# Four small stores and one large load, in place of one large store and four small loads, in a block exchange through DRAM

## The chip, the cores and the metric

The kernel runs on one core of a Trainium2 chip. The metric is the time of the device for one execution, in microseconds (us), the median of several executions. The core has a matrix engine (TensorE, in the profile PE, its weight loads PEld), a vector engine (VectorE, DVE), a scalar engine (ScalarE, ACT), a general engine (GpSimd, POOL) and a queue engine (SyncE, SP), which only issues transfers here. Each of them works through its own instructions strictly in their written order and waits at semaphores for the others. Transfers (DMAs) run on 16 DMA engines of the core, shared by all queues.

## The reference

One transformer block: attention with normalised queries and keys, and then a mixture of experts in which each expert takes its best 512 tokens. Cut to what matters, for `x` of shape 16 x 256 x 256 (batches, tokens, width) and 16 heads of 64:

```python
shift = silu(t) @ W_ada.T + b_ada
h = ln(x, ln1_g, ln1_b) + shift
qkv = (h @ Wqkv.T).reshape(b, n, 3, H, HD)
q = ln(qkv[:, :, 0].transpose(0, 2, 1, 3), qn_g, qn_b)
k = ln(qkv[:, :, 1].transpose(0, 2, 1, 3), kn_g, kn_b)
v = qkv[:, :, 2].transpose(0, 2, 1, 3)
attn = softmax(einsum('bhnd,bhmd->bhnm', q, k) / sqrt(HD))
o = einsum('bhnm,bhmd->bhnd', attn, v)
x = x + o.transpose(0, 2, 1, 3).reshape(b, n, H * HD) @ Wout.T
tok = x.reshape(-1, d)
gate = softmax(tok @ Wgate.T)
vals, idx = top_k(gate.T, bs // E)          # 8 experts, 512 tokens each
g = ln(tok[idx.T], mlp_g, mlp_b)
y = gelu(einsum('ked,ehd->keh', g, fc1s) + b1s)
y = (einsum('keh,edh->ked', y, fc2s) + b2s) * vals.T[..., None]
tok = tok.at[idx.T].add(y)
```

All of it is float32.

## The kernel before

The attention takes the 16 batches one after the other, in a software pipeline with a period of 48.3 us; the mixture of experts follows. In a batch, `First` normalises `x` and transposes it, twelve `Group`s (six column groups of the projection, two halves of the tokens) make queries, keys and values, eight `Quad`s (pairs of head pairs, `d`, each with two steps `i`) do the attention, and two `Tail`s the output projection, the residual, the stores of the tokens and the gate.

Two things have to be transposed between partitions and columns: the normalised keys (`qk` to `kT`) and the softmax rows (`pr` to `prT`). In the first and the last batch (`DIRECT`) TensorE does it. In the 14 batches between, VectorE and the DMA engines do it together, in three steps that the change touches:

- `turn`: VectorE's stream transpose turns each 32 x 32 block within its group of 32 partitions, from `pr` to `pb` (L832; for keys from `qk` to `kb`, L749). Two such instructions fill one tile of 128 partitions by 4 KB, 512 KB in all. The tags `pb` of both kinds share three buffers.
- `away`: SyncE stores the tile to a block in DRAM (`blocks`, L840; `kblocks`, L756).
- `back`: SyncE loads it from there so that the block of rows group `k` and column group `q` ends in row group `q` and column group `k`: four loads, one for each group of 32 partitions, into `prT` (L854) or `kT` (L764).

A batch has eight such exchanges of softmax rows and two of keys: 14 x 8 = 112 and 14 x 2 = 28 in all. Afterwards ScalarE applies gain and bias to the keys in place (`affine`, L770) and TensorE uses them for the scores (L794); `prT` goes into the product with the values (L881).

The order of the work is written out. Each step is added to a `Plan` with an engine; the long list `PLACES` holds a due place for each step, made with an estimate of 0.36 us of SyncE for `away` and 1.6 us for `back`, and the steps are emitted in the order of these numbers. So the order of each engine's instructions is fixed, and each waits for what it needs when its turn comes. SyncE's list holds, beside the exchange, the load of the next batch's `x` (`load_x`, L537, five buffers), the stores of the tokens (`out<-tok`, L918) and of the normalised tokens (`xn_dram<-tn`, L928). VectorE's list holds the statistics of the loaded `x` (`st<-xs`, L610) between the transposes, maxima and scalings of other batches. A transfer that SyncE issues uses one of eight semaphores in turn, so an issue also waits until the transfer eight places before it has landed.

## Time and profile before

| | us |
|---|---|
| median of 3 runs | 1104.83 (1104.45 to 1106.43) |
| profiled execution, whole time | 1106.04 |
| profiled execution, span from first to last instruction | 1104.2 |

| engine | busy us | share of the span |
|---|---|---|
| TensorE, matrix products | 1070.6 | 97% |
| TensorE, weight loads | 714.8 | 65% |
| VectorE | 778.9 | 71% |
| GpSimd | 616.2 | 56% |
| ScalarE | 596.1 | 54% |

The attention takes the first 780 us or so, the selection of the tokens about 60 us, the experts the rest. The granted TensorE clock is 0.99 on average. In the profile's page, a group of instructions is told by its line and by the names of what it writes and reads (`prT<-blocks`). The view of waits sums up, for each engine and line, the idle time just before the instruction and what ended it ("DVE st L610 <- DMA xs<-in_x: 14.2, 5, 3.9": us in total, times, longest). The view by windows gives the busy time of each engine within a stretch, and at the end of a line the granted clock, the mean busy share of the 16 DMA engines and GB/s. The timeline lists instructions in order of time, several alike merged into one row, with idle time and its cause in brackets; times are counted from the start of the span.

### The profile page before, as it was taken

To read this page: it belongs to the slowest core of one execution; us is meant where nothing else is said; L and a number is where in the kernel's file an instruction comes from. 1 tells how busy PE (TensorE), PEld (TensorE's weight loads), DVE (VectorE), ACT (ScalarE), POOL (GpSimd) and SP (SyncE) were. 2 spreads that over 40 slices of the span, in tenths; PEclk is the share of its full clock that TensorE was granted. 3 is DMA by queue.
4 is the path that set the end of the run, shared out by engine and by line. 5 is a ranking of instruction groups with operands and counts; after the bars stand their busy time and mean duration, and the time that the engine had idled before them with its cause. 6 is when DMAs were issued, how large, how long until landed. Compare 5 with 4: busy or idle time off the path is not lost. (4 is left out here: it accounts for less than half of the span.)

```text
span 1104.2 us, 18872 instructions
## 1 busy us (share of the span) xinstructions
PE 1070.6 (97%) x5835; PEld 714.8 (65%) x5835; DVE 778.9 (71%) x2201; ACT 596.1 (54%) x1656; POOL 616.2 (56%) x997
## 2 busy tenths in 40 slices
PE   7999999999999999999899999999988999999996
PEld 4555656566565655656465655656767888888885
DVE  6657888777778777786678787676568488654540
ACT  2768666565766566566557667576522333322331
POOL 3766776776676665675657666565411233333332
PEclk9999999999999999999999999999999999999998
DMA  6013998785888787796787778895130456555661
GB/s 211 1 39 123 277 259 237 230 255 166 248 260 227 226 246 234 201 260 211 211 251 227 228 224 240 243 256 179 63 102 20 113 189 200 170 162 175 196 201 19
DMA packets 147539, 209.20 MB, mean 189 GB/s; under 512 B 15088, under 2 KB 122864, under 8 KB 147440
## 3 DMA queue, kind: packets, MB, share of 16 engines
q1 hardware_dynamic: 139520, 197.71, 60.0%
q0 software_dynamic: 6144, 8.39, 4.1%
q10 hardware_dynamic: 1776, 1.90, 0.5%
q8 instruction: 47, 0.77, 0.3%
q14 instruction: 52, 0.43, 0.1%
HBM read 121.96 MB, written 85.98 MB: 188 GB/s over the span
## 5 line engine op out<-in xcount | busy, mean ns | idle before, releaser
L683 PE MATMUL pm<-wq,hT 128*128 128x512 f32 x768 | 360.4, 605 | 5.0 <-DVE qk L716 2.8
L822 POOL TENSOR_SCALAR pr<-pr,sums 128x256 f32<-128x256 f32 x512 | 237.1, 481 | 112.2 <-DVE sums L818 92.9
L811 ACT ACTIVATE pr<-sc,nmax 128x256 f32<-128x256 f32 x512 | 238.0, 480 | 97.5 <-DVE nmax L802 80.3
L683 PEld LDWEIGHTS pm<-wq,hT 128*128 128x128 f32 x768 | 137.3, 192 | 146.1 <-issue 131.1
L103 POOL TENSOR_TENSOR ss<-ss,neghalf 128x8 f32<-128x8 f32 x128 | 210.5, 1645 | 10.6
L802 DVE TENSOR_REDUCE nmax<-sc 128x2 f32<-128x512 f32 x256 | 165.3, 676 | 16.9 <-PE sc L794 16.3
L832 DVE STREAM_TRANSPOSE pb<-pr 128x512 f32<-128x512 f32 x224 | 149.9, 690 | 18.5 <-POOL pr L822 13.6
L794 PE MATMUL sc<-kT,qT 64*128 64x256 f32 x1024 | 135.4, 397 | 0.0
L881 PE MATMUL po<-prT,v 128*64 128x256 f32 x1024 | 127.6, 388 | 1.1 <-DVE gates L950 1.1
L700 DVE TENSOR_REDUCE ss<-sq 128x8 f32<-128x512 f32 x128 | 86.0, 672 | 47.3 <-ACT sq L696 46.8
L794 PEld LDWEIGHTS sc<-kT,qT 64*128 64x128 f32 x1024 | 92.8, 188 | 40.8 <-issue 25.4
L696 ACT ACTIVATE sq<-pm 128x512 f32<-128x512 f32 x128 | 76.9, 603 | 77.3 <-PE pm L683 75.9
L1301 POOL DMA_INDIRECT out<-y,idx x32 | 51.2, 1601 | 119.8 <-DVE y L1295 66.9
L1268 PE MATMUL ph<-xT,w 128*128 128x256 f32 x512 | 117.6, 383 | 0.0
L907 PE MATMUL pw<-wo,oT 128*128 128x256 f32 x512 | 116.6, 381 | 0.3 <-DVE qk L716 0.3
L1284 PE MATMUL py<-w,hid 128*128 128x256 f32 x512 | 116.3, 380 | 0.0
L716 DVE TENSOR_TENSOR qk<-pm,ss 128x512 f32<-128x512 f32 x128 | 87.0, 681 | 36.9 <-POOL ss L103 35.9
L907 PEld LDWEIGHTS pw<-wo,oT 128*128 128x128 f32 x512 | 96.0, 190 | 23.2 <-issue 9.4
L811 ACT ACTIVATION_READ_ACCUMULATOR pr<-sc,nmax 128x1 f32 x512 | 107.6, 210 | 0.0
L881 PEld LDWEIGHTS po<-prT,v 128*64 128x64 f32 x1024 | 67.1, 137 | 61.5 <-issue 21.1
L1275 ACT ACTIVATE hid<-ph,vec 128x256 f32<-128x256 f32 x128 | 60.4, 474 | 84.2 <-PE ph L1268 76.3
L1284 PEld LDWEIGHTS py<-w,hid 128*128 128x128 f32 x512 | 95.6, 190 | 12.8
(140 smaller groups left out, 1132.6 us busy)
## 6 DMA issues: line engine op xcount, KB each, us to landing
blocks<-pb SPq DMA_DIRECT2D x112, 512.0 KB
prT<-blocks SPq DMA_DIRECT2D x448, 128.0 KB
w<-in_fc2T SPq DMA_DIRECT2D x16, 1024.0 KB
w<-in_fc1T SPq DMA_DIRECT2D x16, 1024.0 KB
kblocks<-kb SPq DMA_DIRECT2D x28, 512.0 KB
kT<-kblocks SPq DMA_DIRECT2D x112, 128.0 KB
out<-tok SPq DMA_DIRECT2D x32, 128.0 KB
xn_dram<-tn SPq DMA_DIRECT2D x32, 128.0 KB
```

Source lines behind the costliest of these rows:

```text
L103: nc.gpsimd.tensor_tensor(dst, src, neghalf[:, : src.shape[1]], ALU.pow)
L683: nc.tensor.matmul(self.pm, hTs[self.b][:, c, bass.ts(self.t, P)], wq[:, c, bass.ts(self.g, GW)], start=(c == 0), stop=(c == DC - 1),)
L716: engine.tensor_tensor(self.qk.rearrange("p (h d) -> p h d", d=HD), src.rearrange("p (h d) -> p h d", d=HD), self.ss[:, 1, :].unsqueeze(2) ...
L794: nc.tensor.matmul(self.sc[i, j][:, t, :], qTs[self.b][rows, hp, bass.ts(t, P)], keys[rows, hp] if direct else keys[rows, hp // 4, hp % 4] ...
L802: nc.vector.tensor_reduce(self.nmax[i, j], self.sc[i, j], AX.X, ALU.max, negate=True)
L811: nc.scalar.activation(self.pr[i, j][:, t, :], self.sc[i, j][:, t, :], AF.Exp, bias=self.nmax[i, j][:, t : t + 1], scale=1.0, accum_out=se ...
L822: nc.gpsimd.tensor_scalar(self.pr[i, j][:, t, :], self.pr[i, j][:, t, :], self.sums[i][:, 1, j, t : t + 1], 1.0, ALU.mult, ALU.mult,)
L832: nc.vector.transpose(self.pb[i][:, :, :, j].rearrange("p k c t n -> p t k c n"), self.pr[i, j].rearrange("p t (k c m) -> p t k c m", c=TB ...
L881: nc.tensor.matmul(self.po[j * HD : (j + 1) * HD, i, :], vs[self.b][:, c, bass.ts(4 * self.d + 2 * i + j, HD)], prT[:, j, c] if self.b in ...
L907: nc.tensor.matmul(self.pw, oTs[self.b][:, hp // 2, self.t, hp % 2, :], wo[:, hp, :], start=(hp == 0), stop=(hp == HP - 1),)
L1268: nc.tensor.matmul(self.ph[f], self.w1[:, c, bass.ts(f, P)], self.xT[:, c, :], start=(c == 0), stop=(c == DC - 1),)
L1284: nc.tensor.matmul(self.py[i], self.hid[:, f, bass.ts(i, P)], self.w2[:, f, :], start=(f == 0), stop=(f == FC - 1),)
```

## The change

The block in DRAM has its dimensions laid out in another order: by the partition that will read it, not by the one that writes it. The shape of the tile stays the same (4 x 32 x 4 x 256 floats). Before, a store writes the 128 partitions one after the other, each 4 KB in one piece, and each of four loads takes for 32 partitions four pieces of 1 KB, 4 KB apart. After, each of four stores writes, for one group of 32 partitions, four pieces of 1 KB that lie 128 KB apart (and 4 KB from the next partition's), and one load reads 128 partitions, each 4 KB in one piece. Both kinds of exchange are changed alike. The planner's numbers and `PLACES` stay, so the order of the steps stays on every engine; within a step of SyncE, `away` has now four transfers and `back` one.

```diff
--- before.py
+++ after.py
@@ -753,17 +753,17 @@
 
             def away(self, kb):
                 self.blocks = dram.tile([QB, SQ, QB, N], F32, tag="blocks", bufs=4, name="kblocks")
+                for k in range(QB):
+                    nc.sync.dma_start(
+                        self.blocks[:, :, k].rearrange("q d n -> d q n"),
+                        kb[0][bass.ts(k, SQ)].rearrange("p q t h m -> p q (t h m)"),
+                    )
+
+            def back(self):
                 nc.sync.dma_start(
-                    self.blocks.rearrange("k d q n -> (k d) (q n)"),
-                    kb[0].rearrange("p q t h m -> p (q t h m)"),
-                )
-
-            def back(self):
-                kT = self.keys()[:, self.g - 2].rearrange("p k t h m -> p k (t h m)")
-                for q in range(QB):
-                    nc.sync.dma_start(
-                        kT[bass.ts(q, SQ)], self.blocks[:, :, q].rearrange("k d n -> d k n")
-                    )
+                    self.keys()[:, self.g - 2].rearrange("p k t h m -> p (k t h m)"),
+                    self.blocks.rearrange("q d k n -> (q d) (k n)"),
+                )
 
             def affine(self):
                 kT = self.keys()[:, self.g - 2].rearrange("p k t h m -> p (k t h m)")
@@ -837,10 +837,11 @@
             def away(self, i):
 
                 self.blocks[i] = dram.tile([QB, SQ, QB, N], F32, tag="blocks", bufs=4, name="blocks")
-                nc.sync.dma_start(
-                    self.blocks[i].rearrange("k m q n -> (k m) (q n)"),
-                    self.pb[i].rearrange("p q c h t n -> p (q c h t n)"),
-                )
+                for k in range(QB):
+                    nc.sync.dma_start(
+                        self.blocks[i][:, :, k].rearrange("q m n -> m q n"),
+                        self.pb[i][bass.ts(k, SQ)].rearrange("p q c h t n -> p q (c h t n)"),
+                    )
 
             def turned(self, i):
                 if i not in self.prT:
@@ -849,11 +850,9 @@
 
             def back(self, i):
 
-                prT = self.turned(i).rearrange("p (k n) -> p k n", k=QB)
-                for q in range(QB):
-                    nc.sync.dma_start(
-                        prT[bass.ts(q, SQ)], self.blocks[i][:, :, q].rearrange("k m n -> m k n")
-                    )
+                nc.sync.dma_start(
+                    self.turned(i), self.blocks[i].rearrange("q m k n -> (q m) (k n)")
+                )
 
             def transposes(self, i, j):
                 self.pp[i, j] = ps.tile([P, TB, N], F32, tag="sc", bufs=4, name="pp")
```

## The prediction

> **What bounds the kernel now.** I read the page's busy table and its slices first, then TensorE's waits, then the tiles of the exchange, and last SyncE's order in time around the few long waits. The page:

> ```profile
> PE 1070.6 (97%) x5835; PEld 714.8 (65%) x5835; DVE 778.9 (71%) x2201; ACT 596.1 (54%) x1656; POOL 616.2 (56%) x997
> DMA  6013998785888787796787778895130456555661
> q1 hardware_dynamic: 139520, 197.71, 60.0%
> q0 software_dynamic: 6144, 8.39, 4.1%
> ```

> TensorE is busy for 97% of the span, so shorter transfers gain only what it still loses to waits; but the 16 DMA engines are 70 to 90% busy in most slices of the attention (to about 780 us), so the changed queue is not idle either. The exchange ends in `prT` (read by TensorE, L881) and `kT` (read by ScalarE, L770). In the view of tile `prT`, the list of what the engines sat idle for has only

> ```profile
>   DMA prT<-blocks: 1.2, 4
>   DMA kblocks<-kb: 0.8, 1
> ```

> that is 2.0 us in 112 + 28 exchanges. By the trace's landing marks (the semaphore updates of each transfer) set against the first read, every `prT` is there at least 2.1 us before its product, half of them over 9.6 us. The exchange itself is covered. What is not covered is a load that the change does not name. VectorE's waits:

> ```profile
> DVE st L610 <- DMA xs<-in_x: 14.2, 5, 3.9
> ```

> The next batch's `x` (L537) is issued by the same SyncE queue, often right behind exchange stores. The timeline of one such place, batch 11's load:

> ```profile
> 419.29 0.34 SPq L756 DMA_DIRECT2D kblocks<-kb  x1
> 419.67 1.27 SPq L840 DMA_DIRECT2D blocks<-pb  x2
> 421.04 1.15 SPq L537 DMA_DIRECT2D xs<-in_x  x1
> ...
> 427.37 0.43 DVE L610 BATCH_NORM_STATS2 st<-xs 128x6 f32<-128x256 f32 x1 [2.06 <-DMA xs<-in_x]
> ...
> 429.25 0.47 ACT L811 ACTIVATE pr<-sc,nmax 128x256 f32<-128x256 f32 x1 [2.04 <-DVE pb L832]
> ...
> 430.58 0.61 PE L944 MATMUL pl<-wg,tokT 128*128 128x8 f32 x4 [1.52 <-ACT tokT L939]
> ```

> Three stores, then the load; VectorE stands 2.06 us for it with two transposes into `pb` queued behind; ScalarE waits 2.04 us for the `pr` that these free; TensorE loses 1.52 us. This is the bound that the change touches.

> **The change, part by part.**

> *Issue on SyncE.* Each exchange keeps five DMAs. Four loads in a row take 1.76 us from first to last (71.63, `kT`), twelve take 5.54 (341.76): 0.46 each. A single store takes 0.34 to 0.43. So each store's place on the queue grows from 0.4 to 1.85 us (+1.4), and each load's shrinks as much. Over a whole exchange SyncE is unchanged; whatever stands between store and load is moved 1.4 us later for each exchange store ahead of it.

> *DMA work.* In windows that hold one kind of transfer, share times length gives its cost in time of all 16 engines:

> ```profile
> 69.70:71.40 1.70, 1.70 (x5) 0.76 (x4) 0.00 (x0) 1.31 (x4) 1.62 (x4) 1.00 0.75 308
> 72.40:75.40 3.00, 3.00 (x15) 1.71 (x14) 1.59 (x3) 1.36 (x3) 2.44 (x4) 1.00 0.62 175
> 272.20:272.90 0.70, 0.70 (x9) 0.35 (x6) 0.70 (x2) 0.00 (x0) 0.62 (x2) 1.00 0.52 187
> ```

> (the last two columns are DMA share and GB/s.) The 512 KB store in 4 KB pieces: 0.75 x 1.70 = 1.28 us. Four loads in 1 KB pieces: 0.62 x 3.00 = 1.86. A 128 KB store in 1 KB pieces (`xn_dram`): 0.52 x 0.70 = 0.36, four of them 1.46. One exchange goes from 3.14 to 1.46 + 1.28 = 2.74 us. The new stores read 32 partitions and write every fourth kilobyte, which no row shows; the lower bound is 1.46, the upper the four loads' 1.86, which have that shape the other way round (3.14: no change). A still dearer price is the last rival. I take 1.46: same direction, same piece.

> *Length of one exchange.* Before: 2.64 us from store to released load (68.99 to 71.63), then 1.76 us of issue and some 2.7 us until the last load's marks: 7.1. After: 1.85 of issue, with 1.3 us from the last store's issue to its landing (marks of lone 128 KB stores: 1.70 from start of issue); then one load, 0.4 + 2.2 + about 0.9 for its further data: 6.7. Within 0.5 us of before, against 2.1 us of cover: nothing for the products. For `kT`, seven of 28 affines stand within 0.2 us of the landing, but scores follow them 0.3 us or more later in all but one. I take -0.5 us for all of this and keep 0 to -2.0.

> [...]

> *Waits.* The product waits for one landing, not four; the load on SyncE and the next VectorE transpose into that `pb` for four, not one. A semaphore instruction takes 21 ns on VectorE and changes no gap between its instructions in the trace: 0. The first products of groups with four landings start after the same 93 ns gap as the direct batches': 0 on TensorE too.

> *What stands behind the stores: the `x` loads.* In batches 9, 10, 12 and 15 no store is directly ahead; in 6 a store and four loads are (now 0.5 us earlier); in 7 and 14 one store (+0.6 and +1.3, slack 0.9 and 2.3). That leaves four:

> - Batch 11: `kblocks` at 419.29, now twelve stores, 5.5 us, so `x` is issued at 424.8, not 421.04. It then landed 6.33 us after issue, because three 512 KB stores were ahead in the DMA engines; now SyncE hands over 0.36 us of work every 0.46 us, so the engines keep up. Lone `x` loads land 2.8 to 3.3 us after issue by the marks, the median of all is 3.7. I take 2.8 to 3.7: 427.6 to 428.5, later by 0.2 to 1.1.
> - Batch 13: `kblocks` at 519.04, same pattern, VectorE released at 527.15: later by 0.2 to 1.1.
> - Batch 8: 275.92, twelve stores and an `out` store, issue at 281.9, landing 284.7 to 285.6 against 283.39: later by 1.3 to 2.2.
> - Batch 5: 131.38, eight stores, issue at 135.1, landing 137.9 to 138.8, against a start of the statistics at 137.19: a new wait of 0.7 to 1.6.

> *From VectorE to TensorE.* The three waits of before, 2.05, 2.06 and 3.94 us, cost TensorE 0.50, 1.52 and 0.56 + 2.23 us: on average the first 1.1 us is absorbed and the rest passes. In batches 8, 11 and 13 the absorbing part is used up, so the addition, 1.7 to 4.4 us, passes whole; batch 5 passes 0 to 0.5. Sum: 1.7 to 4.9, middle 3.3.

> *Sum.* +3.3 - 0.5 = +2.8 us. The profiled execution is 1104.2 of span and 1106.04 in all; it becomes 1108.8. It stands 1.2 above the median of the runs shown, so the median goes from 1104.83 to 1107.6; I say 1107.6.

> **The rivals.**

> - *Covered anyway.* The additions in 11 and 13 come out at their low end and VectorE's lost time is won back at later slack: +0.5 us, 1105.3. For it: the waits are few, and TensorE's stalls total about 10 us in the whole attention. Against: the three existing waits each show in TensorE.
> - *Faster: the queue empties.* The same pacing that delays issue leaves the DMA engines free, the work falls by 0.4 us an exchange, and `x` lands sooner than now. It decides where issue to landing stays under about 2.5 us; then the waits of 11 and 13 shrink, and with the 2.0 us of exchange waits gone the time is about 1102.5, at most 4.8 + 2.0 less: 1098. Against it: no `x` load in the trace lands in under 2.78 us.
> - *Slower by far: 1 KB stores are dear.* The software queue's packets average 4.1% x 16 x 1104.2 / 6144 = 118 ns; if a piece cost that, four stores would take 3.8 us, an exchange 5.1, ten of them 51 us in a batch of 48.3 us. The DMA engines would set the pace: with 0.80 of 48 us used now, some 58 us a batch, over 100 us in all. It decides above about 87 ns a piece (9.4 us free a batch, over ten exchanges of 512 pieces on 16 engines). Against: 1 KB stores on this queue take 0.36 x 16 / 128 = 45 ns.

> [...]

> **How the numbers follow.** Forecast as summed 0.56; covered 0.22; faster 0.15; dear stores 0.07. Differences of under 0.2% (2.2 us) can hardly be measured here. The forecast's own range is 1106 to 1110, a sixth of it within 0.2%. Slower 0.46 + 0.03 + 0.07 = 0.56; same 0.10 + 0.18 + 0.03 = 0.31; faster 0.13. (The covered case gives 0.03 to slower and 0.01 to faster, the faster one 0.03 to the same.) The range goes from 1102.0, just under the faster rival's 1102.5, up to 1112.5, which takes a partial version of the dear stores (TensorE losing the upper 4.9 and `kT` late as well).

> **What would show it.** Right: SyncE rows of four `blocks` stores in 1.8 us; `x` issued near 424.8 and 524.5; VectorE's wait for `xs` up from 14.2 to 17 to 20 us in one more place; TensorE's stalls behind it; DMA busy share of the hardware queue down from 60 to about 55%. Wrong: `xs` waits unchanged or less; packets of the new stores above 60 ns; a `prT` that TensorE waits for.

## The result and the profile after

The changed kernel takes 1116.05 us (median of 4 runs, 1115.19 to 1118.14) against 1105.63 us of the kernel before in the same comparison (4 runs): ratio 1.0097, 95% interval 1.0079 to 1.0116, that is 10.4 us slower. The profiled execution took 1115.93 us, with a span of 1114.0 us (before 1104.2).

The page of the changed kernel, the lines that answer to those shown of before:

```profile
PE 1073.8 (96%) x5835; PEld 714.8 (64%) x5835; DVE 780.6 (70%) x2201; ACT 596.1 (54%) x1656; POOL 618.3 (55%) x997
DMA  6014888785777686777787787876211466556661
q1 hardware_dynamic: 139520, 197.71, 57.8%
```

The DMA engines have less to do: the hardware queue fell from 60.0% of a span of 1104.2 us to 57.8% of one of 1114.0. In time of all 16 engines that is 19 us less, an estimate from these two shares. So the stores in 1 KB pieces are not dear for the DMA engines. TensorE does the same work and is busy 3.2 us longer. The tile `prT` still hides (the list of what the engines sat idle for):

```profile
  DMA blocks<-pb: 1.3, 3
  DMA kblocks<-kb: 0.8, 1
```

The loss shows in the waits (engine, instruction, what it waited for: us in total, times, longest):

```profile
DVE st L610 <- DMA xs<-in_x: 21.8, 7, 5.3
ACT kT L770 <- DMA kT<-kblocks: 16.7, 8, 3.3
DVE pb L832 <- DMA blocks<-pb: 4.8, 7, 1.5
PE pl L943 <- ACT tokT L938: 3.4, 1, 3.4
DVE kb L749 <- DMA blocks<-pb: 2.7, 1, 2.7
PE pl L943 <- DVE gates L949: 2.6, 1, 2.6
```

Before, the first was 14.2 (5 times), and of the others there were

```profile
ACT kT L770 <- DMA kT<-kblocks: 2.5, 3, 1.4
DVE pb L832 <- DMA blocks<-pb: 3.7, 2, 3.2
PE pl L944 <- ACT tokT L939: 1.5, 1, 1.5
```

Two transfers are later than before: the next batch's `x`, as predicted, and the keys' `kT`, to which the prediction had given a small gain. Batch 11's `x` load, the place that the prediction showed:

```profile
425.87 1.77 SPq L757 DMA_DIRECT2D kblocks<-kb  x4
...
427.68 4.02 SPq L841 DMA_DIRECT2D blocks<-pb  x8
...
431.81 0.40 SPq L537 DMA_DIRECT2D xs<-in_x  x1
...
435.41 0.43 DVE L610 BATCH_NORM_STATS2 st<-xs 128x6 f32<-128x256 f32 x1 [3.92 <-DMA xs<-in_x]
...
437.29 0.47 ACT L811 ACTIVATE pr<-sc,nmax 128x256 f32<-128x256 f32 x1 [3.90 <-DVE pb L832]
...
438.63 0.61 PE L943 MATMUL pl<-wg,tokT 128*128 128x8 f32 x4 [3.38 <-ACT tokT L938]
```

Twelve issues take 5.8 us where three took 1.6; the load follows, lands 3.6 us later, and the chain is the one of before with every wait longer. And then comes something that no row of the prediction had: after the pause TensorE runs at half clock. Windows of the same trace (from and to, length, busy time of TensorE, weight loads, VectorE, ScalarE, GpSimd, then the granted clock, DMA share, GB/s):

```profile
286.60:290.04 3.44, 1.65 (x12) 1.21 (x12) 3.32 (x12) 0.59 (x1) 2.23 (x6) 1.00 0.90 291
290.04:293.45 3.41, 3.29 (x16) 1.69 (x16) 3.40 (x8) 2.59 (x9) 3.14 (x5) 0.50 0.96 325
436.80:440.20 3.40, 1.57 (x7) 1.10 (x8) 3.40 (x10) 2.91 (x8) 2.99 (x8) 1.00 0.56 149
440.23:443.64 3.41, 3.41 (x12) 1.20 (x12) 1.62 (x3) 1.04 (x2) 3.24 (x6) 0.50 0.91 207
```

TensorE pauses 2.58 us until 288.02 and 3.38 us until 438.63 (the idle time before its next product), and a stretch of 3.41 us soon behind each pause is granted half clock (0.50), which costs up to 1.7 us of work each (an estimate, half of the 3.41 us). When the starts of the same products are set against each other in the two traces, the changed kernel falls back by 4.1 us at batch 8's `x` load and by 3.5 us at batch 11's, though VectorE waited only 2.33 (4.38 - 2.05) and 1.86 us (3.92 - 2.06) longer there: the rest is about the 1.7 us of the clock. The third largest step, 1.6 us at 505, is no `x` load: just before it VectorE stood 2.7 us for a buffer `pb` that row stores had not yet freed (the fifth line above). Behind `kT` waits the steps are 0.4 to 0.6 us. Past the first 30 us of the attention there are three such half-clock stretches (at 290.0, 440.2 and 542.6), before there was one (at 535.4):

```profile
535.40:538.80 3.40, 3.40 (x17) 2.33 (x14) 2.89 (x5) 1.57 (x6) 2.04 (x5) 0.50 0.48 146
```

### The profile page after: what moved, and what is told of

It reads as the page before. It is cut to its first block, busy times and chain, and to the rows that moved or that the text cites. A ratio compares the mean times of both kernels' runs of the same rounds, so it can differ in the third digit from the quotient of the medians.

```text
span 1114.0 us, 18763 instructions
## 1 busy us (share of the span) xinstructions
PE 1073.8 (96%) x5835; PEld 714.8 (64%) x5835; DVE 780.6 (70%) x2201; ACT 596.1 (54%) x1656; POOL 618.3 (55%) x997
## 3 DMA queue, kind: packets, MB, share of 16 engines
q1 hardware_dynamic: 139520, 197.71, 57.8%
q0 software_dynamic: 6144, 8.39, 4.1%
## 5 line engine op out<-in xcount | busy, mean ns | idle before, releaser
L811 ACT ACTIVATE pr<-sc,nmax 128x256 f32<-128x256 f32 x512 | 238.1, 480 | 98.8 <-DVE nmax L802 73.4
L832 DVE STREAM_TRANSPOSE pb<-pr 128x512 f32<-128x512 f32 x224 | 150.4, 692 | 18.7 <-POOL pr L822 12.1
L880 PE MATMUL po<-prT,v 128*64 128x256 f32 x1024 | 131.2, 396 | 2.8 <-DVE gates L949 2.8
L811 ACT ACTIVATION_READ_ACCUMULATOR pr<-sc,nmax 128x1 f32 x512 | 107.8, 211 | 0.0
```

The source lines that it names most:

```text
L811: nc.scalar.activation(self.pr[i, j][:, t, :], self.sc[i, j][:, t, :], AF.Exp, bias=self.nmax[i, j][:, t : t + 1], scale=1.0, accum_out=se ...
L832: nc.vector.transpose(self.pb[i][:, :, :, j].rearrange("p k c t n -> p t k c n"), self.pr[i, j].rearrange("p t (k c m) -> p t k c m", c=TB ...
L880: nc.tensor.matmul(self.po[j * HD : (j + 1) * HD, i, :], vs[self.b][:, c, bass.ts(4 * self.d + 2 * i + j, HD)], prT[:, j, c] if self.b in ...
```

## The experiments

Two theories stood first. A: the late `x` loads, and the half clock behind the pauses that they cause, carry most of it. B: the exchange itself has become longer, and delays of its loads simply add. In the tables of this section the difference is that of the median to the kernel before in the same comparison.

**One half of the change at a time**, with the order as it is. The rows alone (the keys' `away` and `back` as before; shown are the lines put in, which replace the same lines as in the change):

```diff
+                for k in range(QB):
+                    nc.sync.dma_start(
+                        self.blocks[i][:, :, k].rearrange("q m n -> m q n"),
...
+                    self.turned(i), self.blocks[i].rearrange("q m k n -> (q m) (k n)")
```

and the keys alone:

```diff
+                for k in range(QB):
+                    nc.sync.dma_start(
+                        self.blocks[:, :, k].rearrange("q d n -> d q n"),
...
+                    self.blocks.rearrange("q d k n -> (q d) (k n)"),
```

> The change for the softmax rows alone; the keys' exchange stays as before. Theory A (x loads late behind more issues; a TensorE pause over about 2.1 us is followed by 3.4 us at half clock and costs up to 1.7 us more): only the row stores stand ahead of the x loads, so batch 8's load is issued 1.5 us later than before instead of 2.9, VectorE's wait there is about 3.5 us (before 2.05, after 4.38), TensorE pauses under 2.1 us and the clock does not drop at 290; the same at 440. The late pb buffer at 500 (1.6 us) and the longer waits for the row loads stay. 1108 to 1111 us. Theory B (the one 512 KB load lands later than the last of four 128 KB loads, and SyncE's 8th issue after it waits for that; delays simply add): the rows have two thirds of the exchanges, so 1111 to 1113 us, and this kernel and the one with the keys alone add up to the whole 10.4 us.

> The change for the keys alone; the softmax rows' exchange stays as before. Theory A: batch 8's x load is issued about 1.4 us later than before (kblocks stores 1.77 us in place of 0.32), VectorE's wait there 3.4 us, no clock drop at 290; ScalarE's waits for kT grow to some 10 us in all as in the kernel after (16.7), of which about 1.2 us reaches TensorE: 1107 to 1109 us. The gains of this kernel and of the rows alone add up to clearly less than the whole 10.4 us. Theory B: a third of the exchanges, plus the kT waits: 1108 to 1110 us.

**The x loads out of the way**, in the changed kernel and in the kernel before:

```diff
-            xs[b] = seq.tile([P, TB, D], F32, tag="xs", bufs=5, name=f"xs{b}")
+            xs[b] = seq.tile([P, TB, D], F32, tag="xs", bufs=6, name=f"xs{b}")
...
-        for k in plan.order(PLACES):
+        places = [
+            p - 12.0 if isinstance(st[3], partial) and st[3].func is load_x else p
+            for p, st in zip(PLACES, plan.steps)
+        ]
+        for k in plan.order(places):
```

> The changed kernel with every x load 12 us earlier in SyncE's order, ahead of the kblocks and blocks stores, and one more x buffer. Theory A: VectorE's waits for x (21.8 us) nearly go (under 5 us), with them the TensorE pauses and clock drops at 290, 440 and 542 (4.25 + 3.5 us of the 10.4, and what they cost in the kernel before); the kT waits and the late pb buffer stay: 1103 to 1108 us. Theory B: the waits for x go, but the time stays at 1112 to 1116 us because the loads of prT and kT land as late as before.

> The kernel before with the same edit: x loads 12 us earlier in SyncE's order, one more x buffer. Theory A: VectorE's 14.2 us of waits for x go nearly all; the pauses of TensorE at 430.6 (1.7 us) and 534.5 (2.4 us, and 1.7 us of half clock) go: 1099 to 1103 us. Theory B: x is not what binds in either kernel: 1104 to 1106 us.

| kernel | median us | difference | ratio, 95% interval | waits for x, for kT |
|---|---|---|---|---|
| rows alone | 1114.06 | +9.6 | 1.0075 to 1.0113 | 19.6, 16.0 |
| keys alone | 1112.95 | +8.5 | 1.0064 to 1.0104 | 17.0, 18.4 |
| changed, x early | 1105.99 | +1.5 | 0.9991 to 1.0018 | 5.6, 21.3 |
| before, x early | 1096.78 | -7.7 | 0.9918 to 0.9947 | 5.8, under 1 |

Each half alone costs nearly the whole, above what either theory gave it, so nothing adds up here; B's sum is gone, and so is A's "clearly less". The early `x` loads take 9 to 10 us off the changed kernel (8.9 by the differences, 10.1 by the medians), as A says. But they take 7.7 off the kernel before too, and so the change still costs 9.2 us when no `x` is late at all. A alone is not enough. Most of the waits for `x` are gone in both (what is left, 5.6 us in two places, is the start of the program); ScalarE's waits for `kT` are what differs. SyncE's order at batch 8 with early `x`, before the change:

```profile
274.92 0.32 SPq L756 DMA_DIRECT2D kblocks<-kb  x1
275.29 1.93 SPq L840 DMA_DIRECT2D blocks<-pb  x2
...
279.36 2.07 SPq L764 DMA_DIRECT2D kT<-kblocks  x4
...
284.89 1.24 ACT L770 ACTIVATE kT<-kT,vec 128x1024 f32<-128x1024 f32 x1 [0.57 <-DMA kT<-kblocks]
```

and after it:

```profile
276.45 1.77 SPq L757 DMA_DIRECT2D kblocks<-kb  x4
278.26 4.04 SPq L841 DMA_DIRECT2D blocks<-pb  x8
...
283.35 0.45 SPq L763 DMA_DIRECT2D kT<-kblocks  x1
...
290.36 1.24 ACT L770 ACTIVATE kT<-kT,vec 128x1024 f32<-128x1024 f32 x1 [4.51 <-DMA kT<-kblocks]
...
291.65 2.06 PE L794 MATMUL sc<-kT,qT 64*128 64x256 f32 x8 [3.21 <-ACT kT L770]
```

The `kT` load stands behind the same stores as the `x` load. From the first `kblocks` store to the issue of the load it was 4.4 us, now it is 6.9; from the end of its issue to ScalarE's start it was 3.5, now it is 6.6.

**Issues or pieces?** (theories C and D in the expectations). All three kernels have early `x` loads; the second and the third leave out the exchange itself, as each block comes back to the partitions that it left. The first cuts each store of before in four, with the old layout:

```diff
-                nc.sync.dma_start(
-                    self.blocks[i].rearrange("k m q n -> (k m) (q n)"),
-                    self.pb[i].rearrange("p q c h t n -> p (q c h t n)"),
-                )
+                for k in range(QB):
+                    nc.sync.dma_start(
+                        self.blocks[i][k].rearrange("m q n -> m (q n)"),
+                        self.pb[i][bass.ts(k, SQ)].rearrange("p q c h t n -> p (q c h t n)"),
+                    )
```

(the keys' alike); the second also takes one load in place of four, the third only that:

```diff
-                for q in range(QB):
-                    nc.sync.dma_start(
-                        prT[bass.ts(q, SQ)], self.blocks[i][:, :, q].rearrange("k m n -> m k n")
-                    )
+                nc.sync.dma_start(
+                    self.turned(i), self.blocks[i].rearrange("k m q n -> (k m) (q n)")
+                )
```

> The kernel before with early x loads (1096.8 us), with every one-piece store cut into four of 32 partitions each (4 KB pieces, the layout of before), and the four 1 KB loads kept. What is open: with early x loads the change still costs 9.2 us (1106.0 against 1096.8), and ScalarE's waits for kT go from 0.6 to 21.3 us. Theory C (the three more issues of each store, about 1.4 us of SyncE in order, put the kT load and the next stores behind them): here the same places are 1.4 us longer and the loads not shorter, so at least as late: ScalarE's kT waits 15 us or more, 1104 to 1112 us. Theory D (the size of the pieces, that is 1 KB stores or one 512 KB load of 4 KB pieces, makes the landing late): the stores keep 4 KB pieces and the loads are as before, so kT waits under 5 us and 1096 to 1100 us.

> As the kernel with four stores of 4 KB pieces, and with one load of 4 KB pieces in place of four: the number of issues of the changed kernel, with no 1 KB pieces at all. The exchange itself is left out by this (each block comes back to the partition it left), so the output isn't the reference's; the amount of work is. Theory C (issues): as the changed kernel with early x loads, kT waits 15 us or more, 1103 to 1108 us. Theory D with the store's pieces as the cause: 1096 to 1100 us. Theory D with the one large load as the cause: 1103 us or more here too, and the next kernel decides.

> One store and one load of 4 KB pieces for each exchange, early x loads; the exchange itself is left out as in the kernel just before this one. SyncE issues 420 DMAs fewer than in the kernel before. Theory C (issues): nothing stands longer in SyncE's order than before, so 1094 to 1097 us and kT waits under 2 us. Theory D with the one large load as the cause (it lands 4.5 us after its issue instead of 3.3): kT waits over 8 us and over 1101 us.

| early x, stores and loads | median us | difference | 95% interval of the ratio | waits for kT |
|---|---|---|---|---|
| 1 of 4 KB pieces, 4 of 1 KB (before) | 1096.78 | -7.7 | 0.9918 to 0.9947 | under 1 |
| 1 of 4 KB, 1 of 4 KB | 1096.21 | -9.2 | 0.9905 to 0.9932 | none listed |
| 4 of 4 KB, 1 of 4 KB | 1102.40 | -3.0 | 0.9962 to 0.9990 | 9.8 |
| 4 of 1 KB, 1 of 4 KB (changed) | 1105.99 | +1.5 | 0.9991 to 1.0018 | 21.3 |
| 4 of 4 KB, 4 of 1 KB | 1114.40 | +9.0 | 1.0058 to 1.0087 | 25.9 |

One large load in place of four small ones costs nothing (second row against first, and third against last, where it saves 12.0 us): D's large load is out. Four stores of the old pieces in place of one cost 6.2 us (second to third row, by differences), and the small pieces another 4.5 (third to fourth; 3.6 by the medians, of two comparisons whose runs scatter by 6 to 8 us). So C holds for the larger part, and the store's pieces seem to carry a part that C had denied. In the traces most of that part arises in one place, batch 8's `kT` load, where the kernel with small pieces falls back by another 3.4 us, half of it by a half-clock stretch that the other doesn't have (the eight score products behind the wait take 2.06 us, at full clock 1.13); since such a stretch may come or stay away (see the end), the size of this part is loose. Nor is the step from the second row to the third issue alone, for the DMA engines have more to do as well (second row, then third):

```profile
q1 hardware_dynamic: 79040, 197.68, 50.7%
q1 hardware_dynamic: 85760, 197.71, 56.6%
```

Of spans of 1094.0 and 1101.7 us that is some 0.5 us more of all 16 engines for an exchange. What it does to the keys' exchange can be read from the landing marks: from the first `kblocks` store to the issue of the `kT` load the median grows by 1.8 us (3.0 to 4.8), from there to the landing by 0.4. So most of the delay is in the issues. The change itself has as many transfers as the kernel before and no more work for the DMA engines (60.0% to 57.8%). With four stores and four loads, three more issues in each exchange and more packets too, the kernel loses 16.7 us against the first row; there VectorE also waits 19.2 us for `pb` buffers (7.8 in the changed kernel with early `x`).

**Rows or keys, and the order.** The halves of the change with early `x`, and the changed kernel with early `x` and the keys' loads four units earlier in the written order:

```diff
             p - 12.0 if isinstance(st[3], partial) and st[3].func is load_x
+            else p - 4.0 if getattr(st[3], "__name__", "") == "back" else p
```

> Early x loads, the change for the softmax rows alone (112 of the 140 exchanges; the keys' exchange as before). Both changed and x early is 1106.0 us, none changed 1096.8. If the bunch of row stores ahead of the kT load is what delays it (at 278 us eight issues, 4.0 us, in place of two, 1.9 us): kT waits of 12 us or more, 1102 to 1106 us. If it is the four kblocks stores themselves or the keys' layout: kT waits under 5 us, 1097 to 1100 us.

> Early x loads, the change for the keys alone (28 exchanges). If the rows' stores carry the delay: the kT load is about 1.4 us later at 280 us (four kblocks issues, 1.8 us, in place of 0.3) and kT waits are 5 to 12 us, 1098 to 1102 us; if the keys' own exchange carries it: 12 us or more, 1102 to 1106 us.

> The changed kernel with early x loads (1106.0 us), and the keys' load 4 us earlier in SyncE's order, so that in most groups one row's four stores stand behind it rather than ahead of it. If the kT load standing behind row stores is what costs most of the 9.2 us: ScalarE's kT waits fall from 21.3 us to under 10, the TensorE pause at 291 us (3.4 us, and the half clock behind it) goes, and the time is 1100 to 1103 us, though the row stores are now later and VectorE's waits for a free pb buffer (8.9 us) grow. If the kT load isn't the link, or the row stores pay it all back: 1105 us or more.

Rows alone: 1102.79 us (-2.7; ratio 0.9967 to 0.9985), `kT` waits 17.4. Keys alone: 1102.55 (-3.0; 0.9962 to 0.9984), `kT` waits 16.8. Each costs about 5 us of the 9.2, and each makes `kT` late on its own. SyncE's rows show how: ten of the 28 key exchanges have the stores of two row exchanges between their own store and their load. In the kernel with both halves these ten loads are issued 2.1 to 4.8 us later after their store than before with early `x`, and ten of the twelve `kT` waits follow them; with the rows alone it is 1.1 to 3.1 us. The keys alone put their own three further issues ahead of every `kT` load (1.2 us in the median). The third is slower, not faster: 1111.62 us (+6.1; 1.0048 to 1.0072). Its waits:

```profile
DVE pb L832 <- DMA blocks<-pb: 17.4, 11, 4.0
...
DVE kb L749 <- DMA blocks<-pb: 4.5, 4, 1.8
ACT kT L770 <- DMA kT<-kblocks: 1.4, 3, 1.0
```

The `kT` waits are gone (21.3 to 1.4), as meant. In their place SyncE now stands for the landing of `kblocks` before it can issue the row stores, VectorE waits 21.9 us for `pb` buffers that those stores free (9.6 with the load at its place), and TensorE pauses at 389 and 488 us (4.3 us together), each time with half clock behind it (the mean granted clock of this run is 0.986, and 0.990 with the load at its place). So this other place doesn't mend it: what is moved ahead pushes another transfer out. I take it that SyncE's order is too full at the ends of the batches; other places were not tried.

**What each lateness costs alone.** Batch 8's `x` load 2.3 us later in the kernel before, by tiny loads ahead of it:

```diff
+            for e in range(5 if b == 8 else 0):
+                extra = work.tile([1, 64], F32, tag=f"extra{e}", bufs=1, name="extra")
+                queue.dma_start(extra, x[b * N + e : b * N + e + 1, :64])
```

> The kernel before with five tiny loads (256 bytes each) ahead of batch 8's x load alone, about 2.3 us of SyncE. VectorE's wait there grows from 2.05 to about 4.3 us. If a TensorE pause of over about 2.1 us is followed by half clock: TensorE pauses about 2.7 us near 287 us, the granted clock is near 0.5 to 0.6 for the 3.4 us behind it, and the products from 292 us on are 3.5 to 4.3 us later than before. If only the pause itself counts: 2.0 to 2.6 us later and the clock near 1.

The load was issued 2.5 us later (281.83 against 279.30) but landed only 1.3 later (why was not shown; my guess is that the DMA engines had meanwhile got through the stores ahead); VectorE waited 3.19 us, 1.14 more; TensorE paused 1.26 us with no half clock behind (granted 1.00 from 284 to 296 us), and the products that follow fall back by 1.1 us. Neither expectation was met, as the delay was not, but in this one execution the price is clean: 1.14 us of wait, 1.1 us of time.

Then later `x` loads with nothing else changed, and later `kT` loads with early `x`:

```diff
+            p + 3 if isinstance(st[3], partial) and st[3].func is load_x else p
```

> The kernel before with its exchange untouched and only the x loads later in SyncE's order (three units of the written order, which puts batch 8's and batch 11's behind the four kT loads, some 2.4 to 2.9 us of issue, about what the change does to them). If the late x loads are the cause, as the trace of the changed kernel names them (steps of 4.25 us at batch 8's load and 3.5 at batch 11's): VectorE waits 20 us or more for x in place of 14.2, and the time is 1109 to 1114 us. If they are the small part that the runs with early x loads make them (10.1 us with the change, 8 without it, so about 2 of the 10.4): 1106 to 1108.5 us. In both, ScalarE's waits for kT stay under 5 us.

```diff
+            p + 3 if isinstance(st[3], partial) and st[3].func is load_x and st[3].args[0] in (8, 11, 13) else p
```

> The kernel before with only the x loads of batches 8, 11 and 13 three units later in SyncE's order. From the run with all x loads later (39.8 us more of VectorE's waits for 41.9 us more of time, 1.05 us each): if the late x loads alone can carry most of the 10.4 us, VectorE's waits for x come to 20 to 22 us (21.8 in the changed kernel) and the time to 1111 to 1114 us. If most of such a wait is absorbed, 1106 to 1108 us at the same waits.

```diff
             p - 12.0 if isinstance(st[3], partial) and st[3].func is load_x
+            else p + 2 if getattr(st[3], "__name__", "") == "back" else p
```

> The kernel before with early x loads (1096.8 us) and only the keys' loads two units later in SyncE's order, behind one more row load or store (some 2 us of issue). If late kT loads alone carry most of the 9.2 us: ScalarE's kT waits 15 to 25 us and 1102 to 1106 us. If they are a sign rather than the cause: the same waits and 1097 to 1100 us.

All `x` loads later overshot: 1147.12 us (+41.9; 1.0356 to 1.0407), with 54.0 us of waits. The three alone came close to the size that the change gives them:

```profile
DVE st L610 <- DMA xs<-in_x: 22.5, 6, 6.0
...
ACT kT L770 <- DMA kT<-kblocks: 2.8, 3, 1.5
```

1116.22 us: +12.0 (1.0087 to 1.0129; its profiled execution, at the low end of its runs, has a span 8.2 us longer than before). So 8.3 us more of these waits, without any change of a transfer, cost about as much as the whole change. The total is that of the changed kernel, the lumps are larger: two waits are 3.9 and 2.9 us longer than before, where the change adds 1.2 to 2.3 us in five places, and TensorE pauses 4.04 and 4.44 us there, with one and two steps of half clock behind. So this is nearer to an upper price. The late `kT` loads overshot their size twofold:

```profile
ACT kT L770 <- DMA kT<-kblocks: 43.5, 16, 6.1
PE sc L794 <- ACT kT L770: 14.3, 6, 3.2
DVE st L610 <- DMA xs<-in_x: 7.4, 2, 3.8
```

1123.84 us: +19.6 (1.0143 to 1.0188), 27 us over the kernel with early `x` for 43 us of waits. So late `kT` loads cost time by themselves too, 0.6 us for each us that ScalarE waits.

**What follows.** The change puts three more issues, some 1.4 us of SyncE, ahead of everything that stands behind an exchange store, and at the end of a batch twelve issues where there were three. Two kinds of transfers come late by it, `x` and `kT`, in the same stretches. Either alone would cost nearly what both cost: late `x` alone 8 to 12 us at most for waits of this total, late `kT` and `pb` alone 9.2. They don't add. At batch 8 the traces show why: TensorE pauses there once, in the changed kernel 2.58 us for what hangs on `x`, with `x` early 3.21 us for `kT`. In the later batches that is inferred: with `x` early the pause at batch 11 is gone, and steps of 0.6 to 1.4 us near waits for `kT` and `pb` appear behind its place. The half clock makes the pauses dearer: two more stretches of 3.41 us at half clock than before, 3.4 us of the 9.8 between the two spans. Left open is what the semaphore in turn does: SyncE waited 12.2 us in 14 places at L841 for a `prT` load eight issues before, and no run separates that from the issues themselves.

## Why the prediction was wrong, point by point

The forecast was +2.8 us, from +3.3 for what hangs on `x` and -0.5 for the exchange; +10.4 was measured. The first term was too small, the second had the wrong sign.

- *Bound, and the place of the change.* Right. TensorE bounds the kernel, the rows' exchange stays covered, and the `x` loads behind the stores were what the trace of before could show.
- *Issue on SyncE.* Right: four stores 1.77 us, eight 4.0, one load 0.4.
- *DMA work.* Right in direction, a third in size: 57.8% where about 55% was expected, or 19 us over 140 exchanges, 0.13 us for each in place of 0.40 (an estimate from the two shares). The rival of dear 1 KB stores is refuted by that share.
- *The x loads.* Right in mechanism, a little small. Batch 5: 0.7 to 1.6 was predicted, 1.34 measured. Batch 8: 1.3 to 2.2, measured 2.33. Batches 11 and 13: 0.2 to 1.1 each, measured 1.86 and 1.34. Batch 6: a load 0.5 us earlier was predicted, a wait of 1.23 measured. In all 2.4 to 6.0 was predicted and 8.1 measured (the view's total, which includes the start of the program, grew by 7.6, from 14.2 to 21.8).
- *From VectorE to TensorE: +3.3 us.* Right in how waits pass, wrong in size, for it had no term for the clock. Without the 1.7 us of half clock the steps at batches 8 and 11 are 2.4 and 1.8 us, for 2.33 and 1.86 us of added wait, so these pass whole, as predicted; batch 5's 1.34 us shows no step before the next `kT` wait, and batch 6's 1.23 none, so these are absorbed; batch 13's adds nothing either, where the kernel before had a pause and a half-clock stretch as well. The missing term is 2 x 1.7 us, and the two places alone cost 7.6 us. Where all `x` loads are later, the runs show 1.05 us of time for each us of added wait (41.9 for 39.8), and 1.0 (spans) to 1.45 (medians) where three are. The clock was to be seen in the trace of before, at 535.4 us, behind the longest pause past the start (2.23 us). In the trace of the changed kernel the stretches last 3.41 us and their starts (290.04, 440.23 and 542.62) are 44 and 30 times 3.413 us apart. Pauses of 1.59 and 1.91 us in other runs had half clock behind them too (see the last section).
- *Length of one exchange: -0.5 us.* This step failed with the wrong sign, and it is the deeper error. It built the new length from lone transfers (the last store landed 1.3 us after its issue, the load 3.1), and so found 6.7 us in place of 7.1. For a lone exchange the sign was right: by the landing marks the shortest row exchange goes from 7.16 to 7.02 us. But in the order as it is, the keys' load stands behind up to twelve stores, exactly as the `x` loads do; the row stores land 2.3 us (median) after the end of their issue and the `kT` load 4.7, and the median key exchange, from the first store's issue to the last landing, goes from 9.9 to 10.8 us (with early `x` from 9.6 to 11.0). The prediction had itself counted seven of 28 affines within 0.2 us of the landing; by the same marks 16 of them start within 1.6 us of it. The prediction had written the rule itself, "whatever stands between store and load is moved 1.4 us later for each exchange store ahead of it", and applied it to `x` alone. With `x` out of the way this term is worth +9.2 us, where -0.5 was put.
- *Waits: 0.* Right for the instruction, wrong for what it stands for: a `pb` buffer comes free after four landings, and VectorE waited 8.4 us for such buffers (4.8, 2.7 and 0.9) where it had been 4.3.
- *The range.* Its upper end, 1112.5, was built from "a partial version of the dear stores", with the reason that proved empty; `kT` late is named there in brackets, but no price of it was worked out, and the clock is not in it.

## What to carry to other kernels

Before moving issues within an in-order queue, list everything that stands behind the place that gets longer, not only the transfer that waits today: a covered transfer becomes the next bound by the same few microseconds. The cover that a trace shows is for today's order; take the smallest cover of each transfer on that queue against the whole bunch ahead of it (here twelve issues, not one). And when one late transfer is named by a trace, move it away and look again before giving it the whole loss; here, loading `x` earlier in the kernel before gains 7.7 us (0.7%), and that version, without the change, is the fastest of those that do the whole exchange.

## What the runs showed of the hardware that was not expected

```profile
429.20:432.61 3.41, 1.82 (x8) 0.82 (x7) 3.35 (x11) 1.97 (x7) 2.72 (x7) 1.00 0.48 167
432.61:436.02 3.41, 3.41 (x6) 0.88 (x5) 2.59 (x7) 1.43 (x2) 3.13 (x8) 0.50 0.97 226
```

while in the changed kernel one of 1.92 us (until 505.34) was not, with less of TensorE busy in its step:

```profile
501.67:505.08 3.41, 1.75 (x4) 0.44 (x3) 3.41 (x6) 2.20 (x9) 2.78 (x4) 1.00 0.91 310
505.08:508.49 3.41, 3.15 (x11) 1.72 (x12) 3.17 (x8) 1.66 (x4) 1.36 (x3) 1.00 0.63 217
```

One kernel shows both: with the change for the rows alone, a pause of 1.91 us (until 287.58; 1.50 us of its step busy) is followed by half clock at 288.17, one of 2.25 us (until 435.20; 1.42 us busy) isn't. So neither the pause nor TensorE's busy time in the step decides alone, and what does stays open. The grid of each trace lies elsewhere: its first step within the span begins at 2.9 us before the change and 3.3 after, at 2.5 with batch 8's load delayed and 1.3 with the three loads late (each counted back from a stretch in steps of 3.413 us). So the same kernel might catch one stretch more or fewer, which no run shows, as each kernel has one trace. That may be why the kernels with pauses scatter widely (rows alone 1110.5 to 1117.5 us) and the one without any past the start of the attention doesn't (before with early `x`: 1096.4 to 1097.8); it was not tested. In two places a load that was issued later behind the same stores lost less than the delay: with the five tiny loads ahead, `x` was issued 2.5 us later and landed 1.3 us later, and with the stores in quarters batch 11's took 3.6 us from its issue to VectorE's start where it had taken 6.33, as the prediction had it.
